# Pacing the work behind the scans by TensorE time, in parallel lanes, with a row-shaped norm

## The chip, the cores and the metric

The kernel runs on one core of a Trainium2 chip. The metric is the device time of one execution in microseconds (us). Engines are called by their short names: PE is TensorE (PEld is its weight load), DVE is VectorE, ACT is ScalarE, POOL is GpSimd, SP is SyncE. "Before" took 15,160.82 us in the median of three runs (15,159.55 to 15,173.93).

## The reference, cut to what matters

Four layers follow one another on four images of 192 channels and 64 x 64 points. Layer 0 is a layer norm and two Mamba blocks, layer 1 a norm, one Mamba, a depthwise convolution, a second norm and an MLP; layers 2 and 3 make up what is called stage three below, which the change leaves alone. The parts that count here:

```python
def _mamba(x, in_w, conv_w, ...):
    xz = x @ in_w.T                       # "ps_in": xc and z
    xc, z = jnp.split(xz, 2, axis=-1)
    xc = silu(conv1d(xc) + conv_b)        # "ps_conv"
    dbl = xc @ x_w.T                      # "ps_x": dt, B, C
    dt = softplus(dt @ dt_w.T + dt_b)     # "ps_dt"
    def step(h, inp):
        dA = exp(dt_t * A)                # "dA", one ACT exponential for each scan
        h = dA * h + dt_t * x_t * B_t     # "h", the scans on DVE
        y = einsum('bdn,bn->bd', h, C_t)  # product on POOL, sum on PE ("y")
    y = (ys + D * xc) * silu(z)           # skip on DVE, gate on POOL
    return y @ out_w.T                    # "ps_out"

def _ln(x, g, b):                         # both norms of layer 1
    m, v = mean(x, -1), var(x, -1)
    return (x - m) * rsqrt(v + eps) * g + b
# layer 1: x1 = x + mamba(ln(x)); x2 = x1 + gelu(bn(dw(x1))); x2 + mlp(ln(x2))
```

## The kernel before

A **stretch** is 512 points of one Mamba: 48 scan tiles in 12 groups of four. Stage one (layer 0) has 64 stretches, stage two (layer 1) 32. While DVE scans one stretch, all the other work (norms, projections, convolutions, MLP) is let in between the scan tiles, piece by piece, as Python generators that yield. A *decay* is the tile `dA` that ACT makes for one scan; an *eviction* is ACT's or DVE's reading of a matmul's result out of a `psum` tile; a *burst* is ACT work that needs another function table, let in only at the edge of a group. Before, there was one queue, and each yield counted as one piece, whatever PE time it held:

```python
class Behind:
    def step(self, at_edge):              # one piece of the first entry
        ...
        self.flush()                      # evictions noted by the piece before
        entry = self.queue[0]
        said = next(entry[0])
        ...
# in Scans.run, once for each scan tile i
want = self.credit + self.behind.left / max(1, self.until(r) - r)
while want >= 1:
    if not self.behind.step(edge):
        break
    want -= 1
```

The norm of stage two works with channels on partitions, so mean and variance are sums over partitions, made by PE. The reciprocal root is POOL's power, on a small tile of 128 x 4:

```python
var = self.psum.tile([128, nq], F32, name="var", tag="mm")      # nq = 4
for q in range(nq):
    for k in range(2):
        nc.tensor.matmul(var[:, q : q + 1], sq[:, k, bass.ts(q, 128)],
                         self.mean_w[:, 0:1], start=(k == 0), stop=(k == 1))
rs = self.work.tile([128, nq], F32, name="ln_rs", bufs=2)
nc.scalar.activation(rs, var, AF.Identity, bias=self.eps)
nc.gpsimd.tensor_tensor(rs, rs, self.minus_half, ALU.pow)       # 128 x 4
rb = self.psum.tile([CP, T], F32, name="rb", tag="mm")
for q in range(nq):                                             # spread over partitions
    nc.tensor.matmul(rb[:, bass.ts(q, 128)], rs[:, q : q + 1].to_broadcast([128, CP]),
                     self.ident, start=True, stop=True)
```

Of the kernel before, what the change touches and what calls it, by code (L numbers as in the profile page):

```python
# [20 lines left out]
NB = 4  # L21
# [98 lines left out]

class Behind:
# [4 lines left out]
    def __init__(self):  # L126
        self.queue, self.after, self.left, self.burst = deque(), [], 0, False

    def add(self, gen, n, urgent=False):
        self.left += n  # L130
        if urgent:
            self.queue.appendleft([gen, n])
            self.burst = False
        else:
            self.queue.append([gen, n])

    def later(self, fn):
        self.after.append(fn)

    def flush(self):  # L140
        while self.after:
            fns, self.after = self.after, []
            for fn in fns:
                fn()

    def step(self, at_edge):

        if not self.queue:
            self.flush()
            return False  # L150
        if self.burst and not at_edge:
            self.flush()
            return False
        self.burst = False
        self.flush()
        entry = self.queue[0]
        try:
            said = next(entry[0])
        except StopIteration:
            self.queue.popleft()  # L160
            self.left -= entry[1]
            return True
        if entry[1] > 0:
            entry[1] -= 1
            self.left -= 1
        self.burst = said == "burst"
        return True

    def drain(self):
        while self.queue or self.after:  # L170
            self.step(True)


class NormT:


    N = 9

    def __init__(self, nc, const, work, psum, behind):
        self.nc, self.work, self.psum, self.behind = nc, work, psum, behind  # L180
        self.mean_w = const.tile([CP, CP], F32, name="mean_w")
        nc.vector.memset(self.mean_w, 1.0 / C)
        self.eps = const.tile([128, 1], F32, name="eps")
        nc.vector.memset(self.eps, EPS)
        self.minus_half = const.tile([128, T // 128], F32, name="minus_half")
        nc.vector.memset(self.minus_half, -0.5)
        self.ident = const.tile([128, 128], F32, name="ident")
        make_identity(nc, self.ident)

    def run(self, x, g, b, out):  # L190
        nc = self.nc
        nq = T // 128
        mean = self.psum.tile([CP, T], F32, name="mean", tag="mm")
        for k in range(2):
            nc.tensor.matmul(mean, self.mean_w, x[:, k, :], start=(k == 0), stop=(k == 1))  # L195
        yield
        d = self.work.tile([CP, 2, T], F32, name="ln_d", bufs=1)
        nc.vector.tensor_tensor(d, x, mean.unsqueeze(1).broadcast_to([CP, 2, T]), ALU.subtract)
        yield
        sq = out  # L200
        nc.scalar.activation(sq, d, AF.Square)
        yield
        var = self.psum.tile([128, nq], F32, name="var", tag="mm")
        for q in range(nq):
            for k in range(2):
                nc.tensor.matmul(
                    var[:, q : q + 1],
                    sq[:, k, bass.ts(q, 128)],
                    self.mean_w[:, 0:1],
                    start=(k == 0),  # L210
                    stop=(k == 1),
                )
        yield
        rs = self.work.tile([128, nq], F32, name="ln_rs", bufs=2)
        nc.scalar.activation(rs, var, AF.Identity, bias=self.eps)
        nc.gpsimd.tensor_tensor(rs, rs, self.minus_half, ALU.pow)
        yield
        rb = self.psum.tile([CP, T], F32, name="rb", tag="mm")
        for q in range(nq):
            nc.tensor.matmul(  # L220
                rb[:, bass.ts(q, 128)],
                rs[:, q : q + 1].to_broadcast([128, CP]),
                self.ident,
                start=True,
                stop=True,
            )
        yield
        nc.vector.tensor_tensor(d, d, rb.unsqueeze(1).broadcast_to([CP, 2, T]), ALU.mult)
        yield
        for k in range(2):  # L230
            nc.scalar.activation(
                out[:, k, :], d[:, k, :], AF.Identity, scale=g[:, k : k + 1], bias=b[:, k : k + 1]
            )
        yield


class MlpT:


    N = 12  # L240

    def __init__(self, nc, work, psum, w1, b1, w2, behind):
        self.nc, self.work, self.psum, self.w1, self.b1, self.w2 = nc, work, psum, w1, b1, w2
        self.behind = behind

    def run(self, x, last):
        nc = self.nc
        h = self.work.tile([128, NH, T], F32, name="hid", tag="wide", bufs=1)
        for m in range(NH):
            ps = self.psum.tile([128, T], F32, name="ps_h", tag="mm")  # L250
            for k in range(2):
# [3 lines left out]
            self.behind.later(  # L255
                lambda m=m, ps=ps: nc.scalar.activation(
                    h[:, m, :], ps, AF.Identity, bias=self.b1[:, m : m + 1]
                )
            )
            yield "burst" if m == NH - 1 else None  # L260
        nc.scalar.activation(h, h, AF.Gelu)
        yield
        for k in range(2):
            ps = self.psum.tile([CP, T], F32, name="ps_o", tag="mm")
            for m in range(NH):
                nc.tensor.matmul(  # L266
# [6 lines left out]
                if m == 2:  # L273
                    yield
            self.behind.later(lambda k=k, ps=ps: last(k, ps))
            yield
# [101 lines left out]
class Mamba:  # L378
# [3 lines left out]
    def __init__(self, nc, name, taps, ins, const, work, psum, psum_y, psum_a, dram, ident, ex, behind):  # L382
        self.behind = behind
        self.nc, self.name, self.taps, self.ex = nc, name, taps, ex
        self.work, self.psum, self.psum_y, self.psum_a = work, psum, psum_y, psum_a
# [22 lines left out]

    N = 24

    def front(self, xn, first, u):

        nc, K, later = self.nc, self.taps, self.behind.later
# [4 lines left out]
        z = u["z"] = self.work.tile([128, ND, T], F32, name="z", bufs=2)  # L418
        for e in range(2 * ND):
            ps = self.psum.tile([128, T], F32, name="ps_in", tag="mm")  # L420
            for k in range(2):
                nc.tensor.matmul(  # L422
                    ps, self.in_w[:, k, bass.ts(e, 128)], xn[:, k, :], start=(k == 0), stop=(k == 1)
                )
            to = raw[:, e, K - 1 :] if e < ND else z[:, e - ND, :]
            later(lambda to=to, ps=ps: nc.scalar.copy(to, ps))
            yield
        nc.gpsimd.tensor_copy(self.halo, raw[:, :, T:])
        xc = u["xc"] = self.work.tile([128, ND, T], F32, name="xc", bufs=2)
        for d in range(ND):  # L430
            ps = self.psum.tile([128, T], F32, name="ps_conv", tag="mm")
            for j in range(K):
                nc.tensor.matmul(  # L433
                    ps, self.conv[:, d, j, :], raw[:, d, j : j + T], start=(j == 0), stop=(j == K - 1)
                )
                if j == 1:
                    yield
            later(
                lambda d=d, ps=ps: nc.scalar.activation(
                    xc[:, d, :], ps, AF.Identity, bias=self.conv_b[:, d : d + 1]  # L440
                )
            )
            yield "burst" if d == ND - 1 else None
        nc.scalar.activation(xc, xc, AF.Silu)  # L444
        nc.scalar.activation(z, z, AF.Silu)
        yield
        ps = self.psum.tile([RK + 2 * NS, T], F32, name="ps_x", tag="mm")
# [3 lines left out]
        later(lambda ps=ps: nc.scalar.copy(dbl, ps))  # L451
        yield
        both = self.work.tile([128, 2, ND, T], F32, name="dt_dtx", tag="wide", bufs=1)
        dt, dtx = both[:, 0], both[:, 1]
        for d in range(ND):
            ps = self.psum.tile([128, T], F32, name="ps_dt", tag="mm")
            nc.tensor.matmul(ps, self.dt_w[:, bass.ts(d, 128)], dbl[:RK, :], start=True, stop=True)
            later(
                lambda d=d, ps=ps: nc.scalar.activation(
                    dt[:, d, :], ps, AF.Identity, bias=self.dt_b[:, d : d + 1]  # L460
                )
            )
            yield "burst" if d == ND - 1 else None
        nc.scalar.activation(dt, dt, AF.Softplus)  # L464
        nc.gpsimd.tensor_tensor(dtx, dt, xc, ALU.mult)  # L465
        yield
        rows = []
        for i, v in enumerate((dt, dtx)):
            r = self.dram.tile([DI, T], F32, name=("r_dt", "r_dtx")[i], bufs=3)
# [6 lines left out]
            yield  # L476
        u["C"] = []
        for o in range(2):
            ps = self.psum.tile([128, T], F32, name="ps_C", tag="mm")
            nc.tensor.matmul(ps, self.ex.spread[:, 2 + o, :], dbl, start=True, stop=True)  # L480
            Cs = self.work.tile([128, T], F32, name=f"C{o}", bufs=2)
            later(lambda Cs=Cs, ps=ps: nc.scalar.copy(Cs, ps))  # L482
            u["C"].append(Cs)
            yield
        u["rows"] = rows
        yield
# [16 lines left out]
    def spread(self, u, o):  # L503

        B = u["B", o] = self.psum_a.tile([128, T], F32, name=f"B{o}", bufs=1)
        self.nc.tensor.matmul(B, self.ex.spread[:, o, :], u["dbl"], start=True, stop=True)

# [776 lines left out]
```

## Time and profile before

| what | before |
|---|---|
| time, median of 3 runs | 15,160.82 us |
| a stretch of stage one (64 of them) | 98.48 us |
| a stretch of stage two (32 of them) | 161.66 us |
| from the last of stage one to the first of stage two | 222.8 us |
| from the last of stage two to the end (stage three is most of it) | 3,605 us |

A stretch's length here and below is read from the start times of the first skip addition of each stretch in DVE's timeline: last minus first, over the number of gaps. Where it says "steady", the first four and last two stretches of stage two are left out.

The page cuts the span into 40 slices; each digit is the busy share in tenths, and PEclk is the granted PE clock:

```profile
PE   5666666666666666557776776777677697979799
...
DVE  7888888888889888755556655555654303030210
...
POOL 5667666667666666544434434433443000000000
PEclk7766666766666667667777777777777798989899
```

Stage one is the first 17 slices (DVE mostly at 8), stage two the next 14 (no engine above 7, which means that they wait for each other), stage three the last 9 (PE). The chain that ended last, followed back from the end, by engine:

```profile
PE 37%; POOL 29%; issue 18%; DVE 8%; ACT 5%; DMA 3%; SPq 0%; POOLq 0%; DVEq 0%; ACTq 0%
```

The "POOL 29%" is for the most part the state products of the scans.

### The profile page before, as it was taken

Reading aid. Unit: us, or ns where it says so; the run is one execution under the profiler, and the core shown is the slowest. Engines: PE = TensorE matmul, PEld = TensorE weight load, DVE = VectorE, ACT = ScalarE, POOL = GpSimd, SP = SyncE. Lnnn points to the kernel's source line nnn. Section 1 sums busy time; section 2 is a strip of 40 time slices with the busy share of each in tenths; the row PEclk is TensorE's granted clock in tenths of the full one; section 3 lists DMA queues with packets and bytes.
Section 4 is the critical chain, followed back from the end, with each engine's and each line's share of the span. In section 5 each row is a group of like instructions: output and inputs, shape, how many; then the busy total and the mean of one; then the engine's idle time right before and its main releaser. Section 6 shows DMA issues by size and latency. Waiting matters only on the chain.

```text
span 15172.6 us, 97764 instructions
## 1 busy us (share of the span) xinstructions
PE 10805.9 (71%) x34064; PEld 4671.3 (31%) x34064; DVE 9262.7 (61%) x7740; ACT 6022.3 (40%) x8139; POOL 6543.0 (43%) x3314
## 2 busy tenths in 40 slices
PE   5666666666666666557776776777677697979799
PEld 1222221222222222112222222222222464646465
DVE  7888888888889888755556655555654303030210
ACT  4555555554555555444444444434443111111111
POOL 5667666667666666544434434433443000000000
PEclk7766666766666667667777777777777798989899
DMA  6666666666666666544434434433442100000000
GB/s 137 147 146 149 147 147 148 147 144 148 148 148 151 148 145 150 123 102 101 93 80 99 91 86 94 96 87 80 103 93 57 28 7 11 5 13 5 5 3 7
DMA packets 366755, 1449.43 MB, mean 96 GB/s; under 512 B 95402, under 2 KB 128462, under 8 KB 218710
## 3 DMA queue, kind: packets, MB, share of 16 engines
q1 hardware_dynamic: 365502, 1440.02, 43.5%
q8 instruction: 270, 4.42, 0.1%
q10 hardware_dynamic: 760, 3.16, 0.1%
q14 instruction: 223, 1.83, 0.0%
HBM read 1254.25 MB, written 188.74 MB: 95 GB/s over the span
## 4 chain that ended last, share of the span: by engine, by line
PE 37%; POOL 29%; issue 18%; DVE 8%; ACT 5%; DMA 3%; SPq 0%; POOLq 0%; DVEq 0%; ACTq 0%
POOL h L538 22%; PE plus L1050 6%; PE minus L1050 6%; PE ps_in L422 4%; DVE h L525 3%; PE ps_h L252 3%; PE ps_h L345 2%; PE ps_o L354 2%; PE ps_conv L433 2%; DMA dtxE<-r_dtx 2%; PE ps_o L266 2%; PE y L547 2%; POOL dt_dtx L465 2%; DVE h L510 2%; POOL m_y L564 1%
## 5 line engine op out<-in xcount | busy, mean ns | idle before, releaser
L525 DVE TENSOR_TENSOR_SCAN h<-dA,m_state,h 128x512 f32<-128x512 f32 x4608 | 5622.0, 1267 | 1489.5 <-ACT dA L519 1398.6
L538 POOL TENSOR_TENSOR h<-h,C 128x2048 f32<-128x2048 f32 x1152 | 5203.3, 4517 | 93.4 <-POOL m_state L537 1.6
L519 ACT ACTIVATE dA<-dtE,m_A 128x512 f32<-128x512 f32 x4608 | 3112.6, 688 | 2868.5 <-DVE h L525 2682.8
L547 PE MATMUL y<-h,gather 128*32 128x512 f32 x9216 | 1704.0, 822 | 2100.4 <-POOL h L538 1975.9
L510 DVE TENSOR_TENSOR h<-dtxE,B 128x2048 f32<-128x2048 f32 x1152 | 2603.6, 2260 | 308.0 <-DMA dtxE<-r_dtx 307.5
L537 POOL COPY m_state<-h 128x4 f32<-128x4 f32 x1152 | 215.8, 187 | 2897.9 <-DVE h L525 2851.6
L547 PEld LDWEIGHTS y<-h,gather 128*32 128x32 f32 x9216 | 205.1, 123 | 3288.6 <-POOL h L538 2845.1
L1061 DVE TENSOR_TENSOR y<-plus,neg 96x512 f32<-96x512 f32 x64 | 44.0, 687 | 1600.9 <-ACT neg L1060 1600.9
L1050 PE MATMUL plus<-xn,t 96*96 96x256 f32 x4352 | 1013.6, 380 | 0.0
L422 PE MATMUL ps_in<-xT,m_in_w 96*128 96x512 f32 x1536 | 983.2, 798 | 0.0
L433 PE MATMUL ps_conv<-raw,m_conv 128*128 128x512 f32 x2112 | 952.9, 599 | 0.0
L1050 PE MATMUL minus<-xn,t 96*96 96x256 f32 x3840 | 934.4, 396 | 13.1 <-ACT xn L327 12.8
L449 PE MATMUL ps_x<-xc,m_pack 128*44 128x512 f32 x576 | 454.4, 955 | 650.5 <-ACT xc L444 650.5
L1050 PEld LDWEIGHTS plus<-xn,t 96*96 96x96 f32 x4352 | 710.1, 163 | 338.4 <-issue 133.1
L988 POOL MEMSET img<- 96x132 f32 x4 | 0.8, 204 | 1798.5 <-DVE xw L1035 1798.5
L1050 PEld LDWEIGHTS minus<-xn,t 96*96 96x96 f32 x3840 | 644.0, 170 | 252.4 <-ACT xn L327 29.7
L465 POOL TENSOR_TENSOR dt_dtx<-dt_dtx,xc 128x1536 f32<-128x1536 f32 x96 | 328.8, 3425 | 810.6 <-ACT dt_dtx L464 802.8
L422 PEld LDWEIGHTS ps_in<-xT,m_in_w 96*128 96x128 f32 x1536 | 372.7, 257 | 649.9 <-issue 466.1
L433 PEld LDWEIGHTS ps_conv<-raw,m_conv 128*128 128x128 f32 x2112 | 389.9, 189 | 553.6 <-issue 502.2
L877 PE MATMUL ps_dw<-img,dw 96*96 96x512 f32 x1152 | 550.2, 631 | 14.1 <-ACT C L482 14.1
L195 PE MATMUL mean<-x,mean_w 96*96 96x512 f32 x256 | 236.7, 1079 | 384.0 <-POOL x L899 226.7
L1060 ACT COPY neg<-minus 96x512 f32<-96x512 f32 x64 | 36.7, 573 | 1166.7 <-PE minus L1050 1166.7
(140 smaller groups left out, 11698.4 us busy)
## 6 DMA issues: line engine op xcount, KB each, us to landing
dtE<-r_dt SPq DMA_DIRECT2D x576, 1024.0 KB, 7.3
dtxE<-r_dtx SPq DMA_DIRECT2D x576, 1024.0 KB, 11.3
r_dt<-dt_dtx SPq DMA_DIRECT2D x768, 96.0 KB, 2.9
r_dtx<-dt_dtx SPq DMA_DIRECT2D x768, 96.0 KB, 3.0
x<-x SPq DMA_DIRECT2D x64, 384.0 KB, 3.8
xt<-in_x SPq DMA_DIRECT2D x32, 384.0 KB, 12.3
x<-o SPq DMA_DIRECT2D x32, 384.0 KB, 2.6
img<-x SPq DMA_DIRECT2D x8, 1536.0 KB, 21.6
```

Source lines behind the costliest of these rows:

```text
L252: nc.tensor.matmul(ps, self.w1[:, k, bass.ts(m, 128)], x[:, k, :], start=(k == 0), stop=(k == 1))
L422: nc.tensor.matmul(ps, self.in_w[:, k, bass.ts(e, 128)], xn[:, k, :], start=(k == 0), stop=(k == 1))
L433: nc.tensor.matmul(ps, self.conv[:, d, j, :], raw[:, d, j : j + T], start=(j == 0), stop=(j == K - 1))
L449: nc.tensor.matmul(ps, self.x_w[:, d, :], xc[:, d, :], start=(d == 0), stop=(d == ND - 1))
L465: nc.gpsimd.tensor_tensor(dtx, dt, xc, ALU.mult)
L510: self.nc.vector.tensor_tensor(h, u[k // 2][1], u["B", k % 2].unsqueeze(1).broadcast_to([128, 4, T]), ALU.mult,)
L519: self.nc.scalar.activation(dA, u[k // 2][0][:, j, :], AF.Exp, scale=self.A[:, k, j : j + 1])
L525: self.nc.vector.tensor_tensor_scan(h[:, j, :], u.pop(("dA", k, j)), h[:, j, :], self.state[:, k, j : j + 1], ALU.mult, ALU.add,)
L538: nc.gpsimd.tensor_tensor(h, h, u["C"][k % 2].unsqueeze(1).broadcast_to([128, 4, T]), ALU.mult)
L547: self.nc.tensor.matmul(u["ys"][32 * j : 32 * j + 32, :], self.ex.gather[:, i // 2, :], h[:, j, :], start=(i == 0), stop=(i == 3),)
L877: nc.tensor.matmul(ps, dw[:, k, j, :], img[:, k, r + dy : r + dy + rows, dx : dx + HW], start=(j == 0), stop=(j == 8),)
L1050: nc.tensor.matmul(ps[:, m, :], w["sed"][:, cc, s ^ k, bass.ts(m, CP)], xn[:, cc, bass.ts(s, NWIN)], start=(n == 0 and cc == 0), stop=(n = ...
```

## The change

The intent: DVE should never wait for the work behind it. So that work is put into four lanes, each piece says how much PE time it takes and what has to be done before it, and every scan tile lets in as much as a PE-time budget allows. Evictions come a set number of tiles later. The norm runs a stretch ahead of its use, z is projected last, and stage two's image is kept in three strips instead of one whole tile, so that the queue need not be drained at each image. In the norm, the variance becomes one row. The core of the diff (cuts marked by ...):

```diff
+class Piece:
+    def __init__(self, pe=0.0, wait=0, after=(), burst=False, bank=False, lock=False):
 class Behind:
-    def __init__(self):
-        self.queue, self.after, self.left, self.burst = deque(), [], 0, False
+    BANKS = 2
+    def __init__(self, psum, tile, act, dve, lanes=4):
...
+    def later(self, fn, dve=False, bank=True):
+        self.pending.append((self.now + (self.dve if dve else self.act), fn, done, bank))
...
+    def tick(self, edge):
+        self.now += 1
+        self.issue()
+        self.budget = min(self.budget + self.tile, self.tile)
+        ...                               # lanes in order, while budget is left
+            self.budget -= p.pe
...
 class NormT:
-        var = self.psum.tile([128, nq], F32, name="var", tag="mm")
-        ...                               # 8 matmuls
-        rs = self.work.tile([128, nq], F32, name="ln_rs", bufs=2)
-        nc.scalar.activation(rs, var, AF.Identity, bias=self.eps)
-        nc.gpsimd.tensor_tensor(rs, rs, self.minus_half, ALU.pow)
-        ...                               # 4 matmuls
+        var = behind.bank([1, T], "var")
+        for k in range(2):
+            nc.tensor.matmul(var, self.mean_w[:, 0:1], sq[:, k, :], ...)
+        def power():
+            nc.scalar.activation(rs, var, AF.Identity, bias=self.eps[0:1, :])
+            nc.gpsimd.tensor_tensor(rs, rs, self.minus_half.to_broadcast([1, T]), ALU.pow)
+        h = behind.later(power)
+        yield Piece(0.85, after=[h], wait=4, bank=True)
+        nc.tensor.matmul(rb, self.ones, rs, start=True, stop=True)
...
-        behind = Behind()
+        behind = Behind(psum, 1.85, 2, 3)     # stage one
-        behind = Behind()
+        behind = Behind(psum, 2.1, 1, 2)      # stage two
...
-            img = images[u["b"]]
+            s = strips[b, t] = work.tile([CP, 2, rows + 2, HW + 2], F32, name="strip", bufs=3)
```

`Behind(psum, tile, act, dve)` gives the budget of PE time per scan tile in us, and after how many tiles an eviction by ACT and by DVE is issued.

## The prediction

> **What bounds the kernel now.** I read the page first (its 40 slices show three stages: one that ends near 6,400 us, one that ends near 11,800 us, and a third), then the table of busy time for the middle of each stage:
>
> ```profile
> core 0: us, PE busy (x) PEld busy (x) DVE busy (x) ACT busy (x) POOL busy (x), PEclk, DMA share, GB/s
> 200.00:6400.00 6200.00, 3960.85 (x12048) 1307.48 (x12048) 5501.00 (x4336) 3149.58 (x4440) 4271.06 (x2135) 0.69 0.67 147
> 6650.00:11500.00 4850.00, 3418.39 (x9104) 1257.14 (x9103) 2791.48 (x2111) 2070.63 (x2728) 2027.87 (x1026) 0.76 0.42 92
> 11800.00:15172.00 3372.00, 2990.85 (x11856) 1946.45 (x11856) 640.63 (x972) 562.36 (x651) 2.23 (x9) 0.91 0.04 7
> ```
>
> Columns: stretch, its length, busy us of each engine, granted clock, DMA. Stage one (two Mambas, 64 stretches of 48 scan tiles) keeps DVE 5501/6200 = 89% busy. Stage two (one Mamba, convolution, MLP; 32 stretches) has DVE at 58% and no engine above 70%. Stage three is not touched by the change. From the starts of the first skip addition of each stretch in the timeline, a stretch takes 94 to 102 us in stage one, alternating, mean 98.4; in stage two 160 to 165, with 205 to 210 followed by 137 at each new image.
>
> DVE's floor: four scans and the product ahead of them repeat every 7.09 us in the timeline where nothing waits (6193.41 to 6200.49), so 12 groups take 85.1 us. Three skip additions of 0.65 and about 1.5 us of norm statistics and output additions make 88.5 us in stage one, in accordance with 5501 us over 62 to 63 stretches. In stage two add 4 norm operations of 1.217, 2 additions of 0.689, 2 of 0.745: 95 us. So DVE could give 10 us per stretch in stage one and 67 in stage two.
>
> What takes them in stage one is one row (groups, 1000 to 6000 us):
>
> ```profile
> L525 DVE TENSOR_TENSOR_SCAN h<-dA,m_state,h 128x512 f32<-128x512 f32 x2432 | 2968.2, 1267 | 542.1 <-ACT dA L519 493.4 <-DVE h L510 1.4
> ```
>
> 493.4 us over 50.8 stretches is 9.7 us each: the scan waits for its decay on ACT, and ACT stands in front of an eviction that PE hasn't finished. In stage two DVE's timeline over one start of a stretch shows the shape of the loss:
>
> ```profile
> 8066.22 2.45 DVE L525 TENSOR_TENSOR_SCAN h<-dA,m_state,h 128x512 f32<-128x512 f32 x2
> 8072.84 0.69 DVE L856 TENSOR_TENSOR img<-ps_out,x 96x512 f32<-96x512 f32 x1 [4.17 <-PE ps_out L848]
> 8075.41 0.69 DVE L856 TENSOR_TENSOR img<-ps_out,x 96x512 f32<-96x512 f32 x1 [1.89 <-PE ps_out L848]
> 8083.65 1.22 DVE L198 TENSOR_TENSOR ln_d<-x,mean 96x1024 f32<-96x1024 f32 x1 [7.55 <-PE mean L195]
> 8093.16 1.22 DVE L228 TENSOR_TENSOR ln_d<-ln_d,rb 96x1024 f32<-96x1024 f32 x1 [8.29 <-PE rb L220]
> 8094.30 1.27 DVE L525 TENSOR_TENSOR_SCAN h<-dA,m_state,h 128x512 f32<-128x512 f32 x1
> 8095.49 2.26 DVE L510 TENSOR_TENSOR h<-dtxE,B 128x2048 f32<-128x2048 f32 x1
> 8097.78 1.28 DVE L525 TENSOR_TENSOR_SCAN h<-dA,m_state,h 128x512 f32<-128x512 f32 x1
> 8118.18 2.46 DVE L525 TENSOR_TENSOR_SCAN h<-dA,m_state,h 128x512 f32<-128x512 f32 x2 [19.11 <-ACT dA L519]
> ```
>
> The start of the output projection, a whole norm and a whole Mamba front stand between a few scans: two scans in 50 us. Before this, groups ran at 7.09 us with PE nearly empty. The list of waits (7000 to 11000 us: total, times, longest) says the same of 24.6 stretches:
>
> ```profile
> DVE h L525 <- ACT dA L519: 620.6, 131, 19.3
> ...
> DVE ln_d L198 <- PE mean L195: 385.5, 49, 15.2
> ...
> DVE ln_d L228 <- PE rb L220: 221.9, 30, 8.3
> ...
> DVE x L907 <- PE ps_o L266: 197.4, 30, 11.2
> ```
>
> With 144.3 for a DMA and 121.5 for the output projection these are 1691 us, 69 us per stretch: the whole distance from 93 busy to 162.
>
> **What the Trainium skill says.** "TensorE: Matmul & The Clock Gate", table of specifications: ScalarE, VectorE and GpSimdE take their instructions strictly in order. The trace agrees: scans whose data is there stand behind the 8.29 us wait above. The same page, Part 1: PE's clock is half unless PE has lately been busy. The trace agrees: projection matmul halves start every 0.86 us just after the norm's gaps (8097 us) and every 0.43 us from 8102 us on; so a full 512-column matmul costs 0.86 us warm. "GPSIMD Engine Reference", sections 1 and 3.1: each of 8 cores serves 16 partitions with 16 lanes, and cost goes by the elements of one partition. The trace agrees for a product (below). "ScalarE: Activation LUTs", "What ACT_TABLE_LOAD costs": 1283 ns a load; the trace shows 1283.
>
> **The change, part by part.**
>
> *Order.* By the built order I counted matmuls between the sums of neighbouring groups. Stage two before: 3, 44, 3, 2, 3, 12, 5, 8, 4, 9, 5, 9. After: 5, 7, 9, 9, 9, 8, 8, 6, 1, 11, 8, 8. The lump of 44 (at least 44 x 0.86 = 38 us) is gone; no group carries over 11. A stretch has 89 of them, 77 us warm, and 12 sums of about 1.06 (the new code's own budget; an estimate), 13 us: 90 us of PE against 95 of DVE. ACT evictions come one tile later and DVE ones two (two and three in stage one), so PE should be done when they are reached. The drain of the queue at each image is gone: 205 + 137 - 2 x 162 = 18 to 23 us, three times, 65 us. I followed the scheduler's own bookkeeping while it builds: nothing is forced in mid-stage.
>
> *ACT.* Silu of z becomes a burst of its own: 2 x 1.283 more, 96 times. A burst takes 1.283 + 1.48 + 1.283 = 4.05 us; from the decay before it to the one after it, DVE has three scans and a product, 3 x 1.18 + 2.26 = 5.8 us, against 4.05 + 2 x 0.69 = 5.4. Just hidden, unless evictions stand beside it: some 2 us per stretch in stage one, 5 in stage two (longer Gelu bursts).
>
> *Stage one*: 88.5 + 2 + 1.5 of rest = 92 us. 64 x (98.4 - 92) = 410 us gained.
>
> *Stage two*: DVE 95, ACT 5, PE catching up 5 (it is 90 warm, and not always warm) = 105 us. 32 x (162 - 105) + 65 = 1,890 gained. Prologue and final drain (75 us of PE by the bookkeeping) stay.
>
> *The norm's power.* Stage two's variance was 128 partitions x 4, now one row of 512 on one partition: nine small matmuls fewer for each norm, but the POOL power runs along 512 columns, not 4. The rows of before:
>
> ```profile
> L564 POOL TENSOR_TENSOR m_y<-m_y,z 128x512 f32<-128x512 f32 x288 | 365.9, 1271 | 23.3 <-DVE m_y L558 23.3
> ...
> L216 POOL TENSOR_TENSOR ln_rs<-ln_rs,minus_half 128x4 f32<-128x4 f32 x64 | 64.8, 1012 | 739.2 <-ACT ln_rs L215 739.2
> ```
>
> Products of 512 and 2048 columns (1.271 and 4.517 us) give 0.19 us fixed and 2.1 ns per column. The power of 4 columns has 0.82 us beyond the fixed part. If all that is per column, 0.205 each, a row costs 105 us; if it is mostly fixed, a few us. The trace has no third point. Call it p.
>
> POOL needs 68 us per stretch without powers. A power delays the state products; some 7 us of it is absorbed (the sums stand a tile later, three h buffers). So the stretch is about 105 + 2 x (p - 7) us: p = 15 gives 121, p = 30 gives 151, p = 36 makes stage two as slow as now, and p = 105 makes POOL the bound at 68 + 210 = 278 us or more.
>
> **Sum and rivals.** Small p: 15,161 - 410 - 1,890 = 12,860 us.
> First rival, the power: each us of p beyond 7 costs 64 us. p = 15: 13,370; p = 30: 14,330; p = 105: 12,860 + 32 x (278 - 105) = 18,400 or more. For it: the arithmetic of lanes above. Against it: the new code lets only four tiles pass after the variance before it asks for the power's result, which would be odd if it took tens of us.
> Second rival, PE becomes the bound in stage two: 90 us at full clock, but the granted clock was 0.76. At 0.8 it is 112 us, the stretch 115 or more: 13,200. For it: two PSUM banks make PE wait for evictions. Against: fewer gaps, and stage three has 0.91 at 89% busy.
> Third, ACT bursts undo stage one's gain: 13,270. Fourth, DMA at a faster pace: share 0.67 x 98/92 = 0.71, no bound.
>
> **Range and chances.** The point is the small-p sum with a p of about 15 us, a compromise: 13,400. Low end 12,700: both stages near their floors. High end 16,800: p near 70. I give the power over 45 us a chance of nearly a quarter. Faster by over 2%: 0.67; within 2% (p of some 38 to 48, as p = 43 gives back all 2,300 us): 0.08; slower: 0.25.
>
> **What would show it.** The row of the power, 1x512, is the first to look at. Stage one's stretch should be near 92 with scan waits under 3 us each; stage two's waits of norm operations for PE should be nearly gone and scans even along the stretch, PE clock above 0.8. Scans waiting for POOL or sums for the state product for long in stage two would mean the first rival; PE over 90% busy the second. The prediction is wrong if the power is dear, or if evictions still find PE unfinished.

## The result, and the profile after

The changed kernel took **18,504.17 us** (median of 4 runs, 18,501.95 to 18,505.63) against 15,167.38 us of the kernel before in the same rounds (15,159.55 to 15,179.09): ratio 1.220, 95% interval 1.218 to 1.222, slower. Ratios are the mean time of one kernel's fast runs over that of the other's of the same rounds, so they are not quite the ratio of the medians quoted.

Where it went, from the stretches:

| part | before | after | difference of the whole |
|---|---|---|---|
| stage one, 63 gaps | 98.48 | 92.10 | -402 |
| from stage one to two | 222.8 | 349.8 | +127 |
| stage two, 31 gaps | 161.66 | 270.00 | +3,359 |
| from stage two's last stretch to the end | 3,605 | 3,850 | +245 |

The sum is +3,329 us; the profiled spans differ by 3,327.6. Stage one gained what was hoped; stage two lost eight times as much. The same 40 slices after:

```profile
PE   6777777677776342443343333333434439898989
...
DVE  7999999999998342332332333333323320202020
...
POOL 6777777777776788888888888888788830000000
PEclk7776767777766666666666666666666669898989
```

In the first 13 slices, stage one, DVE is at 9 instead of 8. Then, for some 20 slices, POOL alone is at 8 and PE, DVE and the PE clock fall. The chain that ended last:

```profile
POOL 32%; PE 28%; issue 20%; DVE 11%; ACT 5%; DMA 3%; SPq 1%; POOLq 0%; DVEq 0%; ACTq 0%
POOL ln_rs L265 16%; POOL h L609 12%; DVE h L596 6%; PE plus L1163 5%; PE minus L1163 5%; PE ps_in L472 3%; DVE h L581 3%; PE ps_dw L981 3%; DMA dtxE<-r_dtx 2%; PE ps_h L397 2%; PE ps_o L406 2%; PE ps_conv L490 2%; PE y L618 1%; PE ps_h L301 1%; DVE xw L1148 1%
```

Its lines name a new one in front: "POOL ln_rs", the norm's power. The group (duration in all, mean ns of one | idle time before it, and what ended it):

```profile
L265 POOL TENSOR_TENSOR ln_rs<-ln_rs,minus_half 1x512 f32<-1x512 f32 x64 | 5242.4, 81912 | 282.6 <-ACT ln_rs L264 282.2
```

It is the row that the prediction had said to look at first: one power of 1x512 takes **81.9 us**, where the one of 128x4 had taken 1.0. Busy times of the three stages (length; PE, PEld, DVE, ACT, POOL busy; clock; DMA share; GB/s):

```profile
200.00:5900.00 5700.00, 4057.38 (x11874) 1307.34 (x11872) 5404.21 (x4269) 3267.82 (x4516) 4209.72 (x2103) 0.71 0.71 158
6300.00:14900.00 8600.00, 3288.27 (x8455) 1022.91 (x8454) 2941.21 (x2224) 2220.91 (x2901) 7067.13 (x1162) 0.66 0.24 54
15130.00:18500.00 3370.00, 2994.03 (x11856) 1947.94 (x11856) 640.55 (x972) 562.45 (x651) 2.24 (x9) 0.91 0.04 7
```

Stage one: DVE 5404/5700 = 95% busy, against 89%. Where its gain comes from is seen in DVE's waits from 300 to 5,900 us (total us, times, longest), before:

```profile
DVE h L525 <- ACT dA L519: 548.9, 353, 4.8
```

and after:

```profile
DVE h L581 <- DMA dtxE<-r_dtx: 127.5, 61, 2.9
DVE m_y L629 <- PE y L618: 49.5, 30, 2.0
DVE h L596 <- ACT dA L590: 35.9, 30, 1.2
```

The scans' waits for decays are nearly gone, 9.7 us a stretch before and 0.6 after. Some of that came back as waits for transfers (2.1) and for the sums (0.8). Stage two: POOL 7067/8600 = 82% busy, PE 38%, DVE 34%. No engine is full: the engines take turns. The waits of the whole span (total us, times, longest) say who waits for whom:

```profile
PEld rb L270 <- POOL ln_rs L265: 3007.3, 35, 86.9
PE rb L270 <- POOL ln_rs L265: 2971.9, 35, 86.0
DVE xn L272 <- PE rb L270: 2814.2, 64, 90.0
ACT C L575 <- POOL h L609: 2540.6, 154, 85.6
DVE h L596 <- ACT dA L590: 2499.1, 298, 83.6
```

The timeline over one power, all engines (start, duration; in brackets the idle time before):

```profile
9177.58 81.91 POOL L265 TENSOR_TENSOR ln_rs<-ln_rs,minus_half 1x512 f32<-1x512 f32 x1 [0.97 <-ACT ln_rs L264]
...
9182.78 1.28 ACT L590 ACT_TABLE_LOAD   x1
9184.08 2.73 ACT L590 ACTIVATE dA<-dtE,m_A 128x512 f32<-128x512 f32 x4
9184.80 1.28 DVE L596 TENSOR_TENSOR_SCAN h<-dA,m_state,h 128x512 f32<-128x512 f32 x1 [0.83 <-ACT dA L590]
...
9259.54 2.01 PE L270 MATMUL rb<-ln_rs,ones 1*96 1x512 f32 x2 [85.68 <-POOL ln_rs L265]
...
9261.59 1.22 DVE L272 TENSOR_TENSOR xn<-xn,rb 96x1024 f32<-96x1024 f32 x1 [75.51 <-PE rb L270]
...
9264.04 0.69 ACT L590 ACTIVATE dA<-dtE,m_A 128x512 f32<-128x512 f32 x1 [77.23 <-DVE h L596]
```

These seven lines show one of the two powers of a stretch. It starts at 9177.58. DVE goes on for 8.5 us; then the next thing in its order is the norm's multiplication (L272), which needs `rb` from PE, which needs the power. DVE stands 75.51 us, PE 85.68 (3.7 of it before the power begins), and ACT, whose next decay needs a buffer that the standing scan holds, 77.23. The scans behind L272 need nothing from the norm; they only stand behind it in the same order. By the code they would not have got far, though: `h` has three buffers, and each comes free only after POOL's product, which stands behind the power as well.

The other power of a stretch stops the engines in another way. This is the one before, from the timelines of POOL and DVE:

```profile
9006.27 81.92 POOL L265 TENSOR_TENSOR ln_rs<-ln_rs,minus_half 1x512 f32<-1x512 f32 x1 [7.19 <-ACT ln_rs L264]
...
9094.15 1.28 DVE L596 TENSOR_TENSOR_SCAN h<-dA,m_state,h 128x512 f32<-128x512 f32 x1 [83.64 <-ACT dA L590]
```

Here nobody waits for the norm's result. ACT's copy of C (L575, one buffer) waits 85.56 us for a state product on POOL, which stands behind the power and runs from 9088.41 to 9092.90; the next decays stand behind that copy, and DVE's scan behind the decays. Of the 64 powers, DVE's longest stop beside 36 is at L272 (73 to 90 us), beside the other 28 at a scan or at the clearing of the state (81 to 85 us).

### The profile page after: what moved, and what is told of

The parts are those of the page before. It is cut to its first block, busy times and chain, and to the rows that moved or that the text cites. A ratio compares the mean times of both kernels' runs of the same rounds, so it can differ in the third digit from the quotient of the medians.

```text
span 18500.2 us, 95818 instructions
## 1 busy us (share of the span) xinstructions
PE 10653.7 (58%) x32912; PEld 4382.4 (24%) x32912; DVE 9252.7 (50%) x7741; ACT 6247.2 (34%) x8329; POOL 11740.6 (63%) x3394
## 4 chain that ended last, share of the span: by engine, by line
POOL 32%; PE 28%; issue 20%; DVE 11%; ACT 5%; DMA 3%; SPq 1%; POOLq 0%; DVEq 0%; ACTq 0%
POOL ln_rs L265 16%; POOL h L609 12%; DVE h L596 6%; PE plus L1163 5%; PE minus L1163 5%; PE ps_in L472 3%; DVE h L581 3%; PE ps_dw L981 3%; DMA dtxE<-r_dtx 2%; PE ps_h L397 2%; PE ps_o L406 2%; PE ps_conv L490 2%; PE y L618 1%; PE ps_h L301 1%; DVE xw L1148 1%
## 5 line engine op out<-in xcount | busy, mean ns | idle before, releaser
L265 POOL TENSOR_TENSOR ln_rs<-ln_rs,minus_half 1x512 f32<-1x512 f32 x64 | 5242.4, 81912 | 282.6 <-ACT ln_rs L264 282.2
L618 PE MATMUL y<-h,gather 128*32 128x512 f32 x9216 | 1662.8, 790 | 984.1 <-POOL h L609 956.1
L270 PE MATMUL rb<-ln_rs,ones 1*96 1x512 f32 x128 | 103.2, 898 | 3054.7 <-POOL ln_rs L265 2971.9
L472 PE MATMUL ps_in<-xn,m_in_w 96*128 96x512 f32 x768 | 445.5, 735 | 2316.1 <-ACT C L575 2056.3
L272 DVE TENSOR_TENSOR xn<-xn,rb 96x1024 f32<-96x1024 f32 x64 | 77.9, 1217 | 2814.2 <-PE rb L270 2814.2
L575 ACT COPY C<-ps_C 128x512 f32<-128x512 f32 x192 | 112.5, 586 | 2967.0 <-POOL h L609 2540.6
L472 PE MATMUL ps_in<-xT,m_in_w 96*128 96x512 f32 x1536 | 1035.9, 832 | 61.7 <-ACT z L475 58.0
L472 PEld LDWEIGHTS ps_in<-xn,m_in_w 96*128 96x128 f32 x768 | 172.3, 236 | 2593.3 <-ACT C L575 2080.7
```

Source lines behind the costliest of these rows:

```text
L265: nc.gpsimd.tensor_tensor(rs, rs, self.minus_half.to_broadcast([1, T]), ALU.pow)
L472: nc.tensor.matmul(ps, self.in_w[:, k, bass.ts(e, 128)], xn[:, k, :], start=(k == 0), stop=(k == 1))
L618: self.nc.tensor.matmul(u["ys"][32 * j : 32 * j + 32, :], self.ex.gather[:, i // 2, :], h[:, j, :], start=(i == 0), stop=(i == 3),)
```

## The experiments

My theory after this reading: the row-shaped power alone costs what was lost, about twice 81 us a stretch; the rest of the change gains. Rivals: the new pacing itself delays stage two; or the row form has other costs (broadcast, one partition); or PE would bound stage two in any case.

| run | stage one | stage two | steady | time, us | ratio to before |
|---|---|---|---|---|---|
| before | 98.48 | 161.66 | 164.55 | 15,167 | 1 |
| after | 92.10 | 270.00 | 280.27 | 18,504 | 1.220 |
| e1_power_128x4 | 92.09 | 116.62 | 118.56 | 13,351 | 0.880 |
| e2_old_with_row | 98.48 | 315.61 | 326.54 | 20,348 | one run |
| e5_evict_next_tile | 94.48 | 114.47 | 116.05 | 13,416 | 0.884 |
| e6_ln_exp_edge | 92.06 | 121.91 | 124.48 | 13,510 | 0.890 |
| e7_no_budget | 97.08 | 125.67 | 127.08 | 13,938 | 0.919 |
| e9_z_first | 97.77 | 113.11 | 114.68 | 13,601 | 0.896 |
| e10_power_by_dma | 92.08 | 111.46 | 112.36 | 13,211 | 0.871 |
| e12_dma_z_first | 92.00 | 120.03 | 122.51 | 13,480 | 0.888 |
| e13_power_64_more | 92.04 | 133.57 | 136.55 | 13,855 | 0.913 |
| e14_dma_z_first_evict11 | 92.03 | 122.75 | 124.61 | 13,554 | 0.893 |
| e15_power_16_more | 92.13 | 119.49 | 121.96 | 13,435 | 0.885 |

(Stretches in us from one profiled run each; times are medians. The 95% intervals of the experiments' ratios are 0.0012 to 0.0015 to either side. All runs gave correct results. A further run, of powers of several shapes, is not in the table.)

### The norm's power back at 128 x 4, all else as changed

```diff
-        var = behind.bank([1, T], "var")           # 2 matmuls
+        var = behind.bank([128, nq], "var")        # 8 matmuls
-            nc.gpsimd.tensor_tensor(rs, rs, self.minus_half.to_broadcast([1, T]), ALU.pow)
+            nc.gpsimd.tensor_tensor(rs, rs, self.minus_half, ALU.pow)      # [128, 4]
-        nc.tensor.matmul(rb, self.ones, rs, start=True, stop=True)
+        for q in range(nq): nc.tensor.matmul(rb[:, bass.ts(q, 128)], ..., self.ident, ...)
```

> The changed kernel with the norm's variance and power back in 128 partitions x 4 columns (8 small matmuls for the variance, 4 for the spread-out), same order of everything else. Theory A, the loss is the power's 81.9 us, 64 times, and nothing else: stage two falls from 279 us a stretch to about 105, stage one stays at 92, total 12,860 us (12,700 to 13,200), faster than before by 13 to 16%. Theory B, stage two's new order loses by itself (two PSUM banks for four lanes, PE the bound): stretches of 120 to 150 us and 13,300 to 14,400 us.

Measured: 13,350.69 us (13,344.92 to 13,356.40), ratio 0.8801 (0.8788 to 0.8814). The rest of the change is thus worth 12% and the row took 5,150 us, or 80.5 us for each of the 64 powers; the power itself had grown by 81.9 - 1.0 = 80.9. In the steady part a stretch grew by 280.27 - 118.56 = 161.7 us, for two powers. Busy times of stage one and of stage two in this run, columns as above:

```profile
200.00:5900.00 5700.00, 4048.38 (x11876) 1305.99 (x11874) 5406.30 (x4271) 3274.23 (x4518) 4211.09 (x2104) 0.71 0.71 158
6200.00:9700.00 3500.00, 3120.67 (x9086) 1104.78 (x9085) 2792.29 (x2115) 2104.93 (x2779) 2045.22 (x1101) 0.87 0.56 128
```

Stage one is as in the changed kernel. In stage two PE is 3121/3500 = 89% busy at a granted clock of 0.87, DVE 80%: without the row, PE is the likely bound. That was not tested by itself. That the row is the cause of the loss is shown by this run: without it the new order takes 116.6 us where the old one took 161.7. But theory A's total (12,700 to 13,200) was missed: 13,351 lies in theory B's range, and the stretch between the 105 of A and the 120 to 150 of B. So the new order gains less than was predicted, by 12 to 14 us a stretch. This run also took back the row's matmuls; the run with transfers below keeps them, and shows that it is the power alone that costs.

### The row alone, put into the kernel before

```diff
-        rs = self.work.tile([128, nq], F32, name="ln_rs", bufs=2)
+        rs = out[0:1, 0, :]
+        nc.gpsimd.tensor_tensor(rs, rs, self.minus_half.to_broadcast([1, T]), ALU.pow)
...                                                # var by 2 matmuls, rb by one
```

> The kernel before with one thing of the change: stage two's norm takes variance and power as one row of 512. Theory A: 64 powers of 82 us, in a kernel whose norm is one serial chain in front of the scans, so nearly all is added: 15,160 + 64 x 75 to 81 = 19,900 to 20,400 us. Theory B, the power blocks only in the new order (it is hidden behind the scans in the old): under 17,500 us.

Measured: 20,347.54 us (one run). The steady stretch of stage two went from 164.55 to 326.54, that is by 162.0 us, again two powers in full; stage one did not move (98.48). Theory A's range holds. The row of the power in this run:

```profile
L213 POOL TENSOR_TENSOR xn<-xn,minus_half 1x512 f32<-1x512 f32 x64 | 5242.4, 81913 | 759.6 <-ACT xn L212 756.7
```

So the loss needs nothing of the new scheduler. The old one, which had 67 us of slack on DVE in every stretch, hid none of it either: the slack lay in waits, and a power put into the same chain makes them longer.

### What a POOL power costs, by shape

Twelve instructions on idle tiles were added at the start of e1's kernel: ten powers and two products.

```diff
+        for p, n in ((128, 4), (128, 8), (128, 16), (128, 64), (128, 512), (1, 4), ...):
+            nc.gpsimd.tensor_tensor(pr[:p, :n], pr[:p, :n], ph[:p, :n], ALU.pow)
```

> e1 with twelve POOL instructions at its start, before any work: powers of 128x4, 128x8, 128x16, 128x64, 128x512, 1x4, 1x64, 1x512, 16x64, 32x64, then products of 1x512 and 128x512. Theory A, cost goes by columns alone, 0.37 us + 0.159 us per column whatever the partitions: 1.0, 1.65, 2.9, 10.6, 82, 1.0, 10.6, 82, 10.6, 10.6 us, and products of 1.27 us both. Theory B, a row on one partition is dear because the work isn't spread over the cores: 128x512 far under 82 us (6 to 20) and 1x64 far over 128x64.

Measured (13,536.32 us, one run); the rows by shape, L772 the powers and L774 a product:

```profile
L772 POOL TENSOR_TENSOR probe<-probe,probe_half 128x512 f32<-128x512 f32 x1 | 82.2, 82152 | 0.1
L772 POOL TENSOR_TENSOR probe<-probe,probe_half 1x512 f32<-1x512 f32 x1 | 82.1, 82139 | 0.1
...
L772 POOL TENSOR_TENSOR probe<-probe,probe_half 1x64 f32<-1x64 f32 x1 | 10.5, 10537 | 0.1
...
L772 POOL TENSOR_TENSOR probe<-probe,probe_half 128x16 f32<-128x16 f32 x1 | 2.9, 2901 | 0.1
...
L774 POOL TENSOR_TENSOR probe<-probe,probe_half 1x512 f32<-1x512 f32 x1 | 1.3, 1252 | 0.1
L772 POOL TENSOR_TENSOR probe<-probe,probe_half 128x4 f32<-128x4 f32 x1 | 1.0, 1026 | 0.1
```

Theory A held: one partition or 128 makes no difference; only the columns count. From 512 and 64 columns: (82.15 - 10.55) / 448 = 0.160 us a column, and 10.55 - 64 x 0.160 = 0.3 us fixed. A product of the same row takes 1.25 us. So the power of 128x4 was cheap because it had 4 columns, and turning the same 512 numbers into a row multiplied its length by 80.

### A row without POOL: logarithm and exponential on ACT

```diff
+        yield Piece(after=[h], burst=True)
+        nc.scalar.activation(rs, rs, AF.Ln)                 # [96, 512]
+        nc.scalar.activation(rs, rs, AF.Exp, scale=-0.5)
-            nc.gpsimd.tensor_tensor(rs, rs, ..., ALU.pow)
```

The variance is made with a full matrix of 1/C, so that it stands on all 96 partitions and no `rb` is needed.

> The changed kernel with no power at all: the variance matmul spreads it over 96 partitions, ACT takes exp(-0.5 ln) in one burst at a group's edge, no spread-out matmul. Against e1 (13,351 us; stage two 118 us a stretch with PE 89% busy) PE has some 6.6 us less to do per stretch, ACT some 8.6 us more in two more bursts with table loads. Theory A, PE is what binds stage two after the repair: 113 us a stretch, 13,150 to 13,250 us. Theory B, ACT's bursts bind as much: 13,350 to 13,650 us.

Measured: 13,510.33 us (13,509.66 to 13,512.21), ratio 0.8902. That is 160 us slower than e1: the steady stretch took 124.48 us instead of 118.56, with PE's work about the same (2709/3200 of 124.5 us, 105 us a stretch, against 106). Even so it is 5,000 us faster than the row on POOL. Theory B held. ACT's busy time rose from 71 to 79 us a stretch. The table loads of two more ACT bursts a stretch are the likely price of the 5.9 us, which was not tested apart.

### The row kept, the power done on 128 x 4 after a transfer

```diff
+        nc.sync.dma_start(rs, row)                          # [1, 512] -> [128, 4]
+        nc.gpsimd.tensor_tensor(rs, rs, self.minus_half, ALU.pow)
+        nc.sync.dma_start(back, rs)                         # and back into a row
         nc.tensor.matmul(rb, self.ones[32:33, :], back, start=True, stop=True)
```

> The changed kernel with its rows for variance and spread-out kept (3 matmuls of 512 columns in place of 12 small ones), but the power on 128x4: a small DMA lays the row out over 128 partitions, the power runs, a second DMA brings it back, each a tile or two later. PE has some 2.4 us less per norm than in e1. Theory A, PE binds stage two: 113 us a stretch, 13,130 to 13,260 us. Theory B, it doesn't, or the DMAs' waits stop PE for the result: 13,310 us or more.

Measured: 13,210.80 us (13,204.28 to 13,217.81), ratio 0.8706 (0.8692 to 0.8721): **the fastest of all, 13% under the kernel before**. It keeps what the row was meant to save (nine matmuls less for each norm) and pays two transfers of 2 KB, each 2.0 us from issue to landing in the median; over all 64 norms POOL waited 71 us for the first and PE 27 us for the second. Stage two in this run:

```profile
6300.00:9500.00 3200.00, 2909.68 (x7773) 919.74 (x7771) 2656.30 (x2021) 2038.96 (x2670) 1959.10 (x1055) 0.91 0.60 133
```

PE is busy 2910/3200 = 91% at a clock of 0.91. The stretch fell by 118.56 - 112.36 = 6.2 us, as theory A said, and PE's busy part of it from 106 to 102 (2910/3200 of 112.4). This agrees with PE as the bound of stage two, but does not show it. Busy time times granted clock, an estimate of the work, is 92 us a stretch in e1 and 93 here, so the busy time fell with the clock and not visibly with the work. And there is a rival: in e1 PE stood 119.0 us for the power's result (28 waits from 6,300 to 9,700 us), 4.1 us a stretch, which is most of the 6.2.

### Parts of the new pacing, one at a time

Evictions one tile after their matmuls in both stages, much as in the kernel before:

```diff
-        behind = Behind(psum, 1.85, 2, 3)
+        behind = Behind(psum, 1.85, 1, 1)
-        behind = Behind(psum, 2.1, 1, 2)
+        behind = Behind(psum, 2.1, 1, 1)
```

> e1 with all evictions set one tile after their matmul (stage one had ACT two and DVE three, stage two ACT one and DVE two). Theory A, the later evictions are what took the scans' waits for ACT away in stage one: its stretch goes from 92 back to 95 to 98 us, total 200 to 450 us over e1. Theory B, letting work in by its PE time suffices: within 60 us of e1.

13,416.42 us (13,403.82 to 13,424.46), 66 us over e1: both expectations missed (stage one lost less than the 3 to 6 us of theory A, and stage two gained). In stage one later evictions are worth 94.48 - 92.09 = 2.4 us a stretch; in stage two they cost 2.5 (118.56 against 116.05 steady). No PE-time budget, so that lanes go on as far as banks and waits allow:

```diff
-        behind = Behind(psum, 1.85, 2, 3)
+        behind = Behind(psum, 100.0, 2, 3)
-        behind = Behind(psum, 2.1, 1, 2)
+        behind = Behind(psum, 100.0, 1, 2)
```

> e1 with the PE-time budget per tile taken away in both stages (100 us allowed per tile, so only the two banks, the waits and the burst edges hold work back). Theory A, pacing by PE time is what spreads the work: lumps come back, stage one 94 to 98 us a stretch, stage two over 125, total 13,600 to 14,200 us. Theory B, the two PSUM banks pace the lanes by themselves: within 80 us of e1's 13,351 us.

13,938.28 us (13,937.08 to 13,946.27), within theory A. The budget is worth 5.0 us a stretch in stage one and 8.5 in stage two. z projected right behind xc, with its silu in the same burst:

```diff
+            made.append(project(ND + d, z[:, d, :]))        # ahead of the convolution
+        nc.scalar.activation(z, z, AF.Silu)                  # next to silu(xc)
```

> e1 with z projected right behind the other half again and its Silu in the same burst as the convolution's. ACT saves 96 pairs of table loads (247 us of ACT time), but the double burst takes 5.5 us and with a decay on each side 6.9 us, against 5.8 us that DVE has to do meanwhile. Theory A, z last is worth it for the shorter bursts: 60 to 200 us slower than e1. Theory B, it doesn't matter: within 60 us of 13,351 us, or faster for the ACT time saved.

13,600.74 us (13,590.59 to 13,617.03), 250 us over e1 and so beyond theory A's 200. z last is worth 5.7 us a stretch in stage one and costs 3.9 in stage two. The reason given beforehand, a burst too long for DVE's work, is not what the trace shows: from 300 to 5,900 us DVE's wait for decays grew only from 39.0 us in e1 to 70.1, its wait for the transfer of dt times x (`dtxE`) from 130.5 to 363.1. By the code, z first puts the rows that the scans need later. So two parts of the change that help stage one, where DVE is fullest, harm stage two, where PE is.

### Putting the gains together

If z first and earlier evictions help stage two, they should help e10 as well. z first in stage two only:

```diff
+        for d in range(ND if K == 3 else 0):                 # K == 3: stage two; z ahead of the convolution
...                                                           # z last, with its own burst, only where K == 4
```

> e10_power_by_dma with z projected first in stage two only (last, as before, in stage one). Theory A (z last is a loss in stage two, because its own silu burst and its late projection press on the end of the stretch; the gain seen in e9_z_first adds to that of e10): stage-two stretch down by 3.5 to 4 us from 112.4, stage one stays at 92.1, total 13,090 +- 50 us. Theory B (PE already bounds stage two, and the order of its work no longer matters once the norm is cheap): within 40 us of e10's 13,211.

13,480.33 us (13,466.74 to 13,484.98): **270 us slower than e10**. Both of my expectations missed. Stage one stayed (92.00), the steady stretch of stage two went from 112.36 to 122.51. ACT's waits from 6,300 to 9,500 us have an entry that e10 lacks:

```profile
ACT ln_row L265 <- PE y L633: 256.0, 25, 11.0
```

25 waits in 26 stretches, 256.0 / 25 = 10.2 us each, the size of the loss. ACT's timeline around one of them:

```profile
7592.44 1.91 ACT L605 ACTIVATE dA<-dtE,m_A 128x512 f32<-128x512 f32 x3
7605.32 0.68 ACT L265 ACTIVATE ln_row<-var,eps 1x512 f32<-1x512 f32 x1 [10.96 <-PE y L633]
7605.90 0.67 ACT L605 ACTIVATE dA<-dtE,m_A 128x512 f32<-128x512 f32 x1
```

The row of a norm's variance (L265) is to be copied out on ACT, but PE comes to that variance 11 us late, and the decay behind it (L605) needs nothing from it. It is the same shape of stop as with the power: a norm's piece, set a fixed number of tiles ahead, stands in an engine's order in front of the scans' work. That this wait is the loss is read from its size, not tested. Nor is PE idle in these 11 us: it works without a gap from 7592.60 to 7605, after 3.92 us of waiting for ACT's copy of C, and DVE stands 4.51 us for the MLP's output first. Why PE is late stays open. With earlier evictions in stage two on top:

```diff
-        behind = Behind(psum, 2.1, 1, 2)                      # stage two
+        behind = Behind(psum, 2.1, 1, 1)
```

> e12_dma_z_first with stage two's evictions set one tile later for ACT and one for DVE, as in the kernel before (stage one keeps 2 and 3), and the norm's first transfer asked for a tile sooner. Theory A (the gains of e12 and of stage two's part of e5_evict_next_tile add): 2 us per stretch off e12, total 13,020 to 13,080, the best of all. Theory B (they are the same gain, PE's banks being free sooner): no faster than e12. Theory C (earlier evictions find PE unfinished now that the transfers' waits are tight): slower than e12 by over 40 us.

(The same edit also asks for the power one tile sooner after the first transfer, `wait=1` for `wait=2`. The two were not told apart.) 13,554.15 us (13,550.91 to 13,554.89), another 74 us slower, as theory C said. That wait shrank to 104 us, but DVE now waited for PE (177 us for the MLP's output against 140 in e12, 113 for the mean against 18). Gains of single parts do not add: each was measured in one schedule, and every part moves where the others' pieces fall.

### How much of a short power is hidden

```diff
+            nc.gpsimd.tensor_tensor(
+                self.idle, self.idle, self.minus_half[:, 0:1].to_broadcast([128, 64]), ALU.pow
+            )                                                 # after each norm's power, read by nobody
```

> e1_power_128x4 with one more POOL power of 128x64 (10.53 us in e3_power_shapes) on an idle tile after each norm's power, 64 in all; nobody reads it. The norm doesn't wait for it, only POOL's later products do. My prediction's step (some 7 us of each power is absorbed by later sums and three h buffers): 2 x 3.5 us per stretch, +220 us, 13,570. Rival (nothing is absorbed, every us of a POOL power is added in full as the 2 x 81 us were): +64 x 10.5 = +670 us, 14,020. Third (all of a short one is absorbed, POOL has room): within 60 us of e1's 13,351.

13,855.04 us (13,846.76 to 13,873.95), that is 504 us over e1, 7.9 us for each power of 10.5: between the first two expectations, nearer to the full price (in the steady part (136.55 - 118.56) / 2 = 9.0). The same with 16 columns:

> e13_power_64_more with the extra POOL power at 128x16 (2.90 us in e3_power_shapes) instead of 128x64. The powers of 81.9 us cost 80.5 us each over e1's of 1.0 us (164.9 ms... worked out: (18,504 - 13,351) / 64 = 80.5), the extra ones of 10.5 us cost 7.9 us each (13,855 - 13,351 = 504, / 64). Theory A (the pipeline absorbs a fixed 2 to 3 us of each power, as those two suggest, and adds the rest in full): hidden, within 60 us of e1's 13,351. Theory B (a share of it, some three quarters, is always added): +64 x 2.2 = +140 us, 13,490. The prediction's step (7 us absorbed) says within 60 us too, and has fallen already by e13.

(The "164.9 ms" in that text is a slip of the pen; the working behind it is the one meant.) 13,435.06 us (13,429.99 to 13,441.04), 84 us over e1 by the medians, 73 by the ratios (0.8849 - 0.8801 times 15,180): 1.1 to 1.3 us for each power of 2.9 (1.7 in the steady part). Neither theory was quite right. Of 2.9, 10.5 and 81.9 us, some 1.7, 2.6 and 0.4 us stay hidden (1.2, 1.5 and none in the steady part): at most 3 us, of a POOL that was only 58% busy in stage two of e1. That POOL has time left over does not mean that it has it when the scans' products are due.

## Why the prediction was wrong

It said 13,400 us (12,700 to 16,800), faster with a chance of 0.67. It was 18,504, slower, and out of the range.

**The step that failed is "The norm's power": "The point is the small-p sum with a p of about 15 us, a compromise".** The term p measured 81.9 us. The prediction had the right cue in its hands: the lanes argument (cost goes by the elements of one partition) made 0.205 us a column and 105 us for the row. Against it, it set that the author's four tiles of waiting "would be odd if it took tens of us". A guess about an author's knowledge was weighed against an argument from the profile; then a value between the two was taken for the point, although no argument gave 15 us. The e3 rows show the lanes argument to be right and the size 0.160 us a column.

**The allowance "some 7 us of it is absorbed" failed too.** At most 3 us are (e13, e15), and of the long one practically nothing: the stretch grew by 161.7 us for 2 x 80.9.

**The first rival came within some 100 us ("18,400 or more"), but its sum was not the mechanism.** It made POOL the bound, at 68 + 2p. With the measured p that is 68 + 164 = 232 us, while the steady stretch took 280, and POOL was 82% busy. Nor was it the right one of the prediction's own two sums: at p = 105 the series sum, 105 + 2 x (p - 7), gives 301 us a stretch, longer than POOL's 278, and 19,130 us in all. The power is not what a full POOL spends its time on; it stands in series with everything else, 118.6 + 161.7 us, because DVE, PE and ACT stop for it: for its result in the norm (36 of 64), or for a state product that stands behind it on POOL (28 of 64). At the measured p the series sum gives 105 + 2 x (81.9 - 7) = 255 us. The 25 us that it lacks are 14 of base (118.6 for 105) and 14 for the two allowances of 7, less the 2 us of the two short powers that e1's base holds already. In the rival a p too large and a mechanism too mild made up for each other: that it came near is luck.

**Stage one came out to the tenth:** "88.5 + 2 + 1.5 of rest = 92 us", measured 92.10, and about 400 us gained where 410 were predicted. The cause was right: the scans' waits for decays fell from 548.9 to 35.9 us. The tenth is luck: DVE was busy for 87.3 us of a stretch and not 88.5, the waits for ACT are 0.6 and not 2, and 2.1 us go to waits for transfers, which the sum did not have (the fourth rival had said "no bound"). e5, e7 and e9 show that three parts (evictions 2.4, budget 5.0, z last 5.7) each are needed for the gain; they do not add to the 6.4 us gained in all. The third rival, ACT bursts that undo this gain, did not come.

**"DVE 95, ACT 5, PE catching up 5", together 105 us for stage two, was low by 12 to 14 us**, as e1 shows (116.6, steady 118.6). The likely term is PE, which was 89% busy, 106 us of the stretch, at a granted clock of 0.87. Its work had been counted about right: 106 x 0.87 = 92 us, by the estimate above, against the 90 counted at full clock. What the 105 us left out is the clock: 90 / 0.87 = 103. The second rival named this reason, "At 0.8 it is 112 us, the stretch 115 or more", but with a clock that was not the measured one; that its size fits is in part luck. No run shows PE to be the bound. With p small, the prediction's 12,860 would have been 13,351; that this is near the 13,400 is luck, as that one holds a p of 15 us.

**The lump and the drain** went as predicted: stage two's steady stretches in e1 run between 113 and 123 us, without the 205 us at each image, and DVE's waits of norm operations for PE, 385.5 and 221.9 us from 7,000 to 11,000 us before, are 1.6 and 0.6 from 6,300 to 9,700 us in e1.

## What to carry to other kernels

Before reshaping a tile to save matmuls, look up or measure what its slowest elementwise operation costs by columns: the same 512 numbers cost 1.0 us as 128x4 and 81.9 us as 1x512. When a profile shows one point of a cost curve and the estimates from it differ by a factor of ten, price the whole range, take neither the author's choices as evidence nor the middle as the likely value; here a run of one short probe would have settled it. And an engine's idle share is no room for a long instruction if other engines stand in order behind its result, or behind the work queued after it: 81 us more on a POOL that was 42% idle cost 80.5 us each time.

## What the Trainium skill lacked or had wrong

- "GPSIMD Engine Reference", section 3.1, states about 2.6 cycles per element for a two-input elementwise operation. The runs agree for a product (2048 columns in 4.52 us). The page has no line for the power, which took 0.160 us per column in e3 (10.5 us for 64, 82.2 for 512); at the 1.2 GHz of its section 1 that is an estimate of 192 cycles per element. Nor does it say outright that one row is the worst shape for it: 82.14 us on one partition, 82.15 on 128.
- "ScalarE: Activation LUTs", "What ACT_TABLE_LOAD costs", states a total of some 2.66 us for a switch of tables, of which 1.283 is the load. The changed kernel's trace has the 1.283 us load and no more around it: a Gelu ends at 9182.76 us, the load starts at 9182.78, the next decay at 9184.08.
- No page says how much of a long instruction on one engine is hidden when the others stand in order behind it; here at most 3 us were.
